# Two image layers on one core: spectral factors made on 16 partitions, squares issued at the end of a tick, buffer slots returned one tick later

## The chip, the cores and the metric

The kernel runs on one core of one Trainium2 chip. The engines of a core are PE (TensorE, matrix multiply; its weight loads are shown as PEld), DVE (VectorE), ACT (ScalarE), POOL (GpSimd) and SP (SyncE, which here only issues transfers). The metric is the device time of one execution in microseconds (us), as the median of several runs; less is better.

## The reference

The input is 8 images of 8 channels of 512 x 512, float32. Two layers follow each other, each added to its own input:

```
# layer 0
xs = group_norm(x)[:, :, ::2, ::2]
F  = rfft2(xs)                     # 8 rows (first 4, last 4) x 4 columns are kept
out2[:4 rows]  = einsum('bixy,ioxy->boxy', F[:4 rows],  w1)
out2[-4 rows:] = einsum('bixy,ioxy->boxy', F[-4 rows:], w2)
x = x + real(out2 . E1(X) . E2(T)) / 256**2    # E: complex exponentials

# layer 1, on v = group_norm(x)
grid = v
repeat 15 times:
    mapped = 3.9 * grid * (1 - grid)
    grid = 0.85 * (0.7 * mapped + 0.3 * conv3x3(mapped, K)) + 0.15 * v
cml = clip(grid, 0.0001, 0.9999)
nca = sigmoid(conv1x1(relu(conv3x3(v, Wp)), Wu))           # 128 hidden channels
g   = sigmoid(conv1x1(relu(conv3x3([v, cml, nca], Wg1)), Wg2))
x = x + g * cml + (1 - g) * nca
```

## The kernel before, in words

Everything is unrolled, and each engine keeps the order in which the source issues its instructions (`keep_order`). Time is cut into ticks: `work` (L889) issues one tick, 75 of them for each image, after a prologue that makes layer 0 of image 0. A tick holds work of several images at once: the 15 coupled steps and the hidden layer (`nca`) of image b, the gates of image b-1, and layer 0 (`layer0`, the spectral part) of image b+1. The last image has no successor, and after it only hidden rounds and gates are left.

**The steps.** A `Half` is four of the eight channels of an image. The 512 rows are covered by 19 overlapping slabs of 32 rows; five sets (k = 0 to 4) of four slabs each make a half. A tick does two (set, step) pairs, numbered n within the half: pair n is set n % 5 at step n // 5 + 1. The 75 pairs of the first half are followed directly by those of the second, and those by the next image's. `convolve` (L528) does a set's 3 x 3 convolution on PE: 48 matrix multiplies, 96 in the trace, in 3.3 us, so two sets are 192 instructions (L533). `settle` (L582) reads the result with DVE (L588), adds the drive term and squares on ACT (L594), in two pieces of two banks. The four pairs of PSUM banks turn between the two sets, the hidden rounds, and the others.

**What a half needs at its start.** Each set has two arrays of drive values, dE and dO (1 MB each, four transfers each, L491), and a state m. `fetch` (L506) issues the loads, from 11 pairs ahead of the half's start on, in the order k, then dE before dO, for as long as there are loads left and a slot is free. `square` (L510) makes the first m of a set from dE: POOL writes two border columns (L512), ACT squares 2048 columns (L513, 1.99 us). For set k it is issued in the tick that holds pair k - 2. `prepare` and `drive` (L526, POOL) scale dO and dE.

**Slots.** dE, dO and m share 15 slots of a pool, handed out first in, first out (`Slots`, L138). A drive is given back by `settle` at steps 14 and 15. At step 15 `leave` (L565) clips m on DVE (L568) and puts `store` off to the end of the tick (`later(1, ...)`, run by `tick`, L171): four transfers of the finished rows to `cml` (L574), after which the slot of m is given back at once. Who takes such a slot next, a load on SP or a memset on POOL, waits for the stores to land.

**The order within a tick** (L889 to L912): `prepare` of the halves; the two sets' `convolve` and `settle`; the gates' `finish`; `transfers`, which issues the loads of gates (`feed`), of x for layer 0, and of the halves (`fetch`); one or two hidden rounds (L633 on PE, ACT L639 and DVE L641, each on half of the result); then `squares`; then one slot of "others" (a gate's convolution L703 or a piece of layer 0), the hidden layer's point convolution every second round (L652; its result is copied to y by ACT, L659, or added by DVE, L661, and finished by ACT's sigmoid, L665), another slot of "others" (a gate's second convolution L720 or a piece of layer 0); then `tick`, which issues what was put off.

**The spectral part.** `layer0` is a generator of pieces. It projects the subsampled image with matrix multiplies on a table of cosines and sines (L336, `dft_y`, with the image as weights), normalises the sums (L350, L353), projects again (L361) to 8 partitions (one for each wave number along one axis), and mixes the channels on DVE with the weights `wmix` (`total`, L369; results `re` and `im`). The way back multiplies with e1, whose partitions 0 to 7 hold the cosines and 8 to 15 the sines. Its factors `om` therefore have 16 partitions. DVE writes the first 8 (L387, L388) and a small tile `of_sin` (L389, L390), which a transfer of 2 KB carries to partitions 8 to 15 (L391, on SP's queue). `over_rows` (L398) multiplies om by e1; ACT copies the result to ty (L402); `synthesis` (L430, L433) ends the way back. All SP transfers are issued in the order of the source; an issue that must wait holds up those behind it.

Of the kernel before, what the change touches and what calls it, by code (L numbers as in the profile page):

```python
# [35 lines left out]
F32 = mybir.dt.float32  # L36
AF = mybir.ActivationFunctionType
ALU = mybir.AluOpType
# [3 lines left out]
P = 128  # L42
C = 8
# [42 lines left out]
def shape_constants():  # L86

    ky = np.array([0, 1, 2, 3, -4, -3, -2, -1])
    kx = np.arange(4)
    c = {}  # L90
    p, j = np.arange(P)[:, None, None], np.arange(2)[None, :, None]
    a = 2 * np.pi * ((ky * (2 * p + j)) % NS) / NS
    c["dft_y"] = np.concatenate([np.cos(a), -np.sin(a)], axis=2)
    a = 2 * np.pi * ((kx * (P * j + p)) % NS) / NS
    re = np.concatenate([np.cos(a), -np.sin(a)], axis=2)
    im = np.concatenate([np.sin(a), np.cos(a)], axis=2)
    c["dft_x"] = np.stack([re, im], axis=2)
    waves = np.zeros((8, 4))
    waves[:, 0] = ky / NS
    waves[:, 1] = np.concatenate([kx, -kx]) / NS  # L100
    waves[:4, 2] = 0.25
    c["waves"] = waves
    i, o = np.arange(P)[:, None] % SLAB, np.arange(SLAB)[None, :]
    c["shift"] = np.stack([i - o == d - 1 for d in range(3)], axis=1)
    p = np.arange(P)
    c["ends"] = np.stack([p % SLAB == 0, p % SLAB == SLAB - 1, p == 0, p == P - 1], axis=1)
    c["group_of"] = (np.arange(P)[:, None] % C) // 2 == np.arange(G)[None, :]
    return {k: np.ascontiguousarray(v, dtype=np.float32) for k, v in c.items()}
# [18 lines left out]
def conv_layers(ctx: ExitStack, tc: tile.TileContext, a, out):  # L127
# [50 lines left out]
    def load(name, shape):  # L178
        t = cp.tile(shape, F32, name=name)
        nc.scalar.dma_start(out=t, in_=a[name])  # L180
        return t
# [7 lines left out]
    xs_first = [load_x(sets, 0, c) for c in range(C)]  # L189


    dft_y = load("dft_y", [P, 2, 16])
    dft_x = load("dft_x", [P, 2, 2, 8])
    waves = load("waves", [8, 4])
    group_of = load("group_of", [P, G])
    ends = load("ends", [P, 4])
    w_p = load("w_p", [P, 3, 2, HID])
# [18 lines left out]

    e1 = cp.tile([16, N], F32, name="e1")
    e2 = cp.tile([P, N], F32, name="e2")
    om = cp.tile([16, C, 32], F32, name="om")
    nc.gpsimd.memset(om, 0.0)  # L220
    grid = {}
    for name in "XT":
# [3 lines left out]
    def sines():  # L226
        u, k, t = (sets.take([8, N], name) for name in ("u", "k", "sines"))
        rd = sm.tile([8, 1], F32, name="rd")
        for to, name, col, shift in (
            (e1[:8], "X", 0, 0.25), (t, "X", 0, 0.0), (e2[:8], "T", 1, waves[:, 2:3])  # L230
        ):
            xr = grid[name]
            nc.vector.tensor_tensor(rd, xr[:, 2:3], xr[:, 0:1], ALU.subtract)
            nc.vector.reciprocal(rd, rd)
            nc.vector.tensor_tensor(rd, rd, waves[:, col : col + 1], ALU.mult)
            nc.vector.tensor_scalar(u, xr, rd, shift, ALU.mult, ALU.add)
            nc.vector.tensor_scalar(k, u, MAGIC, None, ALU.add)
            nc.vector.tensor_scalar(k, k, MAGIC, None, ALU.subtract)
            nc.vector.tensor_tensor(u, u, k, ALU.subtract)
            nc.scalar.activation(to, u, AF.Sin, scale=6.283185)  # L240
        nc.scalar.dma_start(out=e1[8:], in_=t)
        for j in range(1, 4):
            nc.scalar.dma_start(out=e2[32 * j : 32 * j + 8], in_=e2[:8])
        for tile_ in (u, k, t, *grid.values()):
            sets.drop(tile_)
# [72 lines left out]
    def layer0(e, bank):  # L318


        def one():
            return bank[-1][:, 0]

        st = sm.tile([P, C, 4, 6], F32, name="st")
        mys = sm.tile([P, C, 2, 16], F32, name="mys")


        for c in range(C):
            yield c
            xt = e.x[c]  # L330
            for j in range(4):
                nc.vector.bn_stats(st[:, c, j], xt[:, j])
            my = one()[:, :32].rearrange("p (h k) -> p h k", h=2)
            for h in range(2):
                for j in range(2):
                    nc.tensor.matmul(  # L336
                        my[:, h], xt[:, 2 * j, h * NS : (h + 1) * NS : 2], dft_y[:, j],
                        start=(j == 0), stop=(j == 1),
                    )
            nc.scalar.copy(mys[:, c], my)  # L340
            e.done_with(c)
# [6 lines left out]
        for g in range(G):  # L348
            at = mys[:, 2 * g : 2 * g + 2]
            nc.vector.tensor_scalar(  # L350
                at[:, :, :, 0], at[:, :, :, 0], lift[:, g : g + 1], None, ALU.subtract
            )
            nc.vector.tensor_scalar(at, at, rstd[:, g : g + 1], None, ALU.mult)  # L353
        wmix, ts = row([8, 2, C, C, 4], "wmix"), row([8, 2, C, C, 4], "ts")
        nc.sync.dma_start(out=wmix, in_=a["wmix"])
        yield LATER
        mx = one()[:, : C * 8].rearrange("p (c k) -> p c k", k=8)
        for c in range(C):
            for h in range(2):
                for q in range(2):  # L360
                    nc.tensor.matmul(  # L361
                        mx[:8, c], mys[:, c, h, q * 8 : (q + 1) * 8], dft_x[:, h, q],
                        start=(h + q == 0), stop=(h + q == 2),
                    )
        f = sm.tile([8, C, 2, 4], F32, name="f")
        nc.vector.tensor_copy(f, mx[:8].rearrange("p c (q k) -> p c q k", q=2))


        def total(q0, v0, q1, v1, op, name):  # L369
            for i, (q, v) in enumerate(((q0, v0), (q1, v1))):  # L370
                nc.vector.tensor_tensor(
                    ts[:, i], f[:, :, q].unsqueeze(2).to_broadcast([8, C, C, 4]), wmix[:, v],
                    ALU.mult,
                )
            nc.vector.tensor_tensor(ts[:, 0], ts[:, 0], ts[:, 1], op)
            t = sm.tile([8, C, 4], F32, name=name)
            nc.vector.tensor_reduce(t, ts[:, 0].rearrange("k i o m -> k o m i"), AX.X, ALU.add)
            return t

# [2 lines left out]
        yield LATER  # L382
        im = total(0, 1, 1, 0, ALU.add, "im")

        of_sin = sm.tile([8, C, 8], F32, name="of_sin")
        s = 1.0 / (NS * NS)
        nc.vector.tensor_scalar(om[:8, :, 0:4], re, s, None, ALU.mult)  # L387
        nc.vector.tensor_scalar(om[:8, :, 4:8], im, s, None, ALU.mult)  # L388
        nc.vector.tensor_scalar(of_sin[:, :, 0:4], im, -s, None, ALU.mult)  # L389
        nc.vector.tensor_scalar(of_sin[:, :, 4:8], re, s, None, ALU.mult)  # L390
        nc.sync.dma_start(out=om[8:, :, :8], in_=of_sin)  # L391
        yield LATER


        def over_rows(c):
            ps = one()
            for at in range(0, P, 32):
                nc.tensor.matmul(  # L398
                    ps[at : at + 32], om[:, c], e1, start=True, stop=True, tile_position=(0, at)
                )  # L400
            ty = row([P, P, 4], "ty")
            nc.scalar.copy(ty.rearrange("k p j -> k (p j)"), ps)  # L402
            return ty
# [68 lines left out]
    class Half:  # L472
# [31 lines left out]
                    self.square(k)  # L504

        def fetch(self, n):  # L506
            while n >= -11 and self.loads and (self.loads[0][2] or sets.free):
                self.load(nc.sync)

        def square(self, k):  # L510
            m = self.m[k] = sets.take([P, 4, NP], "m")
# [53 lines left out]
    def leave(m, k, half):  # L565

        g = m[:, :, 1 : N + 1]
        nc.vector.tensor_scalar(g, g, 0.0001, 1.0 - 0.0001, ALU.max, ALU.min)  # L568

        def store():  # L570
            for h in range(4):
                s = 4 * k + h
                lo, hi = SHARES[s]
                nc.sync.dma_start(  # L574
                    out=half.cml[1 + STARTS[s] + lo : 1 + STARTS[s] + hi, half.c0 : half.c0 + 4],
                    in_=g[32 * h + lo : 32 * h + hi],
                )
            sets.drop(m)

        later(1, store)  # L580

# [307 lines left out]
    def work(sets, rounds, e, after, transfers, squares=lambda: None):  # L889

        settled = iter(())
        for (half, step, k), ps in zip(sets, (pairs[:2], pairs[2:])):
            convolve(half.m[k], half.c0, step - 1, ps)
            next(settled, None)
            settled = settle(half, step, k, ps)
            next(settled)
            others.finish()
        others.finish()
        transfers()
        for ps in (pairs[:2], pairs[2:])[:rounds]:  # L900
            e.hidden.round(ps, after, settled)
        next(settled, None)
        squares()

        a, b, c, d = (pairs[i] for i in ((0, 1, 3, 2), (2, 0, 3, 2))[rounds == 1])

        point = rounds and e.hidden.n % 2 == 0
        others.first([a, b if point else c])
        if point:
            e.hidden.point(c[:, 0])  # L910
        others.second([d if point else c])
        tick()  # L912

    elements = [e]
    for n in range(-FIRST_ROUNDS, 0, 2):
# [99 lines left out]
```

## Time and profile before

| | |
|---|---|
| median of 3 runs | 9992.99 us (9989.27 to 10003.49) |
| the profiled execution | 9988.58 us; its span, first to last instruction, 9986.8 us |
| granted TensorE clock, mean | 0.983 of full |
| HBM | 992.27 MB read, 268.78 MB written, 126 GB/s over the span |

In the rows of the profile, a group is given as line, engine, operation, tiles written and read, shape and count; then busy us, mean ns of one; then the engine's idle time just before, and what ended most of it. In the views of waits each row has the us in total, the times, and the longest. In the timeline each row has start and length in us, engine, line, operation, count, and in brackets the idle time before it and what ended it. "issue" there means that the engine waited for nothing that the profile shows. PE's matrix multiplies overlap each other and their ends are modelled.

### The profile page before, as it was taken

Reading aid. Unit: us, or ns where it says so; the run is one execution under the profiler, and the core shown is the slowest. Engines: PE = TensorE matmul, PEld = TensorE weight load, DVE = VectorE, ACT = ScalarE, POOL = GpSimd, SP = SyncE. Lnnn points to the kernel's source line nnn. Section 1 sums busy time; section 2 is a strip of 40 time slices with the busy share of each in tenths; the row PEclk is TensorE's granted clock in tenths of the full one; section 3 lists DMA queues with packets and bytes.
Section 4 is the critical chain, followed back from the end, with each engine's and each line's share of the span. In section 5 each row is a group of like instructions: output and inputs, shape, how many; then the busy total and the mean of one; then the engine's idle time right before and its main releaser. Section 6 shows DMA issues by size and latency. Waiting matters only on the chain. (4 is left out here: it accounts for less than half of the span.)

```text
span 9986.8 us, 353049 instructions
## 1 busy us (share of the span) xinstructions
PE 9359.6 (94%) x160496; PEld 4296.7 (43%) x160496; DVE 5869.1 (59%) x6067; ACT 4297.8 (43%) x4445; POOL 1755.5 (18%) x1406
## 2 busy tenths in 40 slices
PE   6999999899998999989999899999999899998999
PEld 2444444443444444444444444444434444444433
DVE  5665555665566655666556655566555565555555
ACT  2444444444444434444344443444434354344422
POOL 2010111103121031101312013120121202211212
PEclk9999999999999999999999999999999999999999
DMA  4241355447544565445665356552566526753688
GB/s 147 88 120 34 82 140 134 134 127 168 139 128 136 126 163 137 133 124 135 159 144 141 112 141 162 141 158 94 143 160 145 155 91 144 168 129 94 150 199 200
DMA packets 625562, 1353.48 MB, mean 136 GB/s; under 512 B 73066, under 2 KB 73194, under 8 KB 594050
## 3 DMA queue, kind: packets, MB, share of 16 engines
q1 hardware_dynamic: 621728, 1329.77, 52.0%
q8 instruction: 1261, 20.66, 0.9%
q14 instruction: 235, 1.93, 0.1%
q10 hardware_dynamic: 2338, 1.13, 0.0%
HBM read 992.27 MB, written 268.78 MB: 126 GB/s over the span
## 5 line engine op out<-in xcount | busy, mean ns | idle before, releaser
L533 PE MATMUL pair<-m,band 32*32 32x512 f32 x115200 | 4096.7, 605 | 200.2 <-issue 96.0
L594 ACT ACTIVATE m<-m 128x1024 f32<-128x1024 f32 x2240 | 2363.7, 1055 | 2795.7 <-DVE m L588 2674.2
L533 PEld LDWEIGHTS pair<-m,band 32*32 32x32 f32 x115200 | 2262.4, 103 | 1941.3 <-issue 970.0
L633 PE MATMUL pair<-cols,w_p 32*128 32x511 f32 (+1 forms) x24576 | 2866.2, 603 | 41.4 <-DMA cols<-xn 14.2
L588 DVE SCALAR_TENSOR_TENSOR m<-pair,dO 128x1024 f32<-128x1024 f32 x1280 | 1507.2, 1219 | 1478.0 <-PE pair L533 1294.2
L633 PEld LDWEIGHTS pair<-cols,w_p 32*128 32x128 f32 x24576 | 1270.8, 186 | 1651.0 <-issue 1123.3
L588 DVE SCALAR_TENSOR_TENSOR m<-pair,dE 128x1024 f32<-128x1024 f32 x1120 | 1319.1, 1219 | 1068.6 <-PE pair L533 878.3
L641 DVE TENSOR_SCALAR h<-pair,b_p 128x1024 f32<-128x1024 f32 x1024 | 1312.9, 1283 | 810.8 <-PE pair L633 803.3
L639 ACT ACTIVATE h<-pair,b_p 128x1024 f32<-128x1024 f32 x1024 | 1140.3, 1114 | 1043.4 <-PE pair L633 1043.0
L652 PE MATMUL pair<-h,w_u 128*32 128x512 f32 x8192 | 996.5, 598 | 136.4 <-DVE h L641 123.5
L726 POOL TENSOR_TENSOR mix<-mix 96x512 f32<-96x512 f32 x344 | 437.4, 1271 | 3757.9 <-ACT mix L724 3551.2
L703 PE MATMUL pair<-gin,w_g 128*32 128x511 f32 (+1 forms) x8256 | 964.1, 600 | 33.3 <-DMA gin<-nca 17.0
L708 POOL TENSOR_TENSOR mix<-mix 96x512 f32<-96x512 f32 x344 | 443.4, 1289 | 2050.6 <-DMA mix<-nca 1340.1
L598 POOL TENSOR_SCALAR dO<-dO 128x2048 f32<-128x2048 f32 x80 | 431.9, 5410 | 1225.6 <-DVE m L588 1225.5
L652 PEld LDWEIGHTS pair<-h,w_u 128*32 128x32 f32 x8192 | 249.4, 110 | 757.1 <-issue 384.0
L703 PEld LDWEIGHTS pair<-gin,w_g 128*32 128x32 f32 x8256 | 235.3, 110 | 711.2 <-issue 472.2
L665 ACT ACTIVATE y<-y,b_u 128x512 f32<-128x512 f32 x256 | 184.7, 721 | 808.0 <-DVE y L661 807.8
L731 DVE SCALAR_TENSOR_TENSOR mix<-mix,back 96x512 f32<-96x512 f32 x344 | 335.7, 976 | 148.5 <-POOL mix L726 148.5
L659 ACT COPY y<-pair 128x512 f32<-128x512 f32 x256 | 149.7, 585 | 605.1 <-PE pair L652 482.8
L713 DVE TENSOR_SCALAR mix<-pair,b_g 128x512 f32<-128x512 f32 x344 | 258.0, 750 | 251.6 <-PE pair L703 251.4
L720 PE MATMUL pair<-mix,w_g 128*32 128x512 f32 x2064 | 356.8, 593 | 9.6 <-DVE mix L713 7.8
L526 POOL TENSOR_SCALAR dO<-dO,base 128x512 f32<-128x512 f32 x320 | 237.0, 756 | 453.8 <-DMA dO<-xn 323.0
(86 smaller groups left out, 2643.8 us busy)
## 6 DMA issues: line engine op xcount, KB each, us to landing
gin<-xn SPq DMA_DIRECT2D x344, 384.0 KB
cols<-xn SPq DMA_DIRECT2D x256, 512.0 KB
x<-in_x SPq DMA_DIRECT2D x120, 1024.0 KB
gin<-cml SPq DMA_DIRECT2D x344, 320.0 KB
gin<-nca SPq DMA_DIRECT2D x344, 320.0 KB
dE<-xn SPq DMA_DIRECT2D x320, 256.0 KB
dO<-xn SPq DMA_DIRECT2D x320, 256.0 KB
mix<-xn SPq DMA_DIRECT2D x344, 192.0 KB
```

The source lines that it names most:

```text
L533: nc.tensor.matmul(ps[h // 2][32 * t : 32 * t + 32, h % 2], band[at, c0 + (t if step % 2 else h), dx], m[at, t, dx : dx + N], start=(n == ...
L588: nc.vector.scalar_tensor_tensor(u[:, at], ps[q], FLOOR, d[:, at], ALU.max, ALU.add)
L594: nc.scalar.square(u[:, at], u[:, at])
L598: nc.gpsimd.tensor_scalar(d, d, 0.5, None, ALU.add)
L633: nc.tensor.matmul(ps[g // 2][:, g % 2, lo:hi], w_p[p, dx, i % 2], self.cols[p, i // 2, at : at + hi - lo], start=(n == 0), stop=(n == 2), ...
L639: nc.scalar.activation(h[:, :2], ps[0], AF.Relu, bias=b_p)
L641: nc.vector.tensor_scalar(h[:, 2:], ps[1], b_p, 0.0, ALU.add, ALU.max)
L652: nc.tensor.matmul(ps[32 * g : 32 * g + 32], w_u[:, r % 4], h[:, g], start=(r == self.hs[0][0]), stop=(r == self.hs[-1][0]), tile_position ...
L703: nc.tensor.matmul(ps[32 * j : 32 * j + 32, lo:hi], gband[:, dx], gin[:, j, at : at + hi - lo], start=(n == 0), stop=(n == 2), tile_positi ...
L708: nc.gpsimd.tensor_tensor(d, d, ng, ALU.subtract)
L720: nc.tensor.matmul(ps[at], gpoint[:, at], mix[:, 3], start=True, stop=True, tile_position=(0, 32 * j),)
L726: nc.gpsimd.tensor_tensor(d, d, mix[: GR * C, 2], ALU.mult)
```

## The change

Four things are changed.

1. The cosine and sine columns of `dft_y` stand twice, so both projections give their results on 16 partitions, the second 8 a copy of the first. `wmix` comes twice as well. `om` is then written whole by DVE, in four operations with per-partition scale factors (two more columns in `waves`) that are zero on one half of the partitions; the tile `of_sin` and its transfer are gone. `om` holds 8 columns for each channel in place of 32, and the matrix multiply reads 32 columns from there on, of which the first 8 are used.
2. The slot of a stored m is given back one tick after its stores are issued.
3. `squares` is called after `tick` in place of after the hidden rounds.
4. `fetch` issues at most 8 loads for each half and tick.

```diff
-    c["dft_y"] = np.concatenate([np.cos(a), -np.sin(a)], axis=2)
+    c["dft_y"] = np.concatenate([np.cos(a), np.cos(a), -np.sin(a), -np.sin(a)], axis=2)
...
-    waves = np.zeros((8, 4))
-    waves[:, 0] = ky / NS
-    waves[:, 1] = np.concatenate([kx, -kx]) / NS
+    waves = np.zeros((16, 5))
+    waves[:8, 0] = ky / NS
+    waves[:8, 1] = np.concatenate([kx, -kx]) / NS
     waves[:4, 2] = 0.25
+    waves[:8, 3] = 1.0 / (NS * NS)
+    waves[8:, 4] = -1.0 / (NS * NS)
...
-    om = cp.tile([16, C, 32], F32, name="om")
+    om = cp.tile([16, C + 3, 8], F32, name="om")
...
-        mys = sm.tile([P, C, 2, 16], F32, name="mys")
+        mys = sm.tile([P, C, 2, 32], F32, name="mys")
...
-            my = one()[:, :32].rearrange("p (h k) -> p h k", h=2)
+            my = one()[:, :64].rearrange("p (h k) -> p h k", h=2)
...
-                at[:, :, :, 0], at[:, :, :, 0], lift[:, g : g + 1], None, ALU.subtract
+                at[:, :, :, 0:9:8], at[:, :, :, 0:9:8], lift[:, g : g + 1], None, ALU.subtract
...
-        wmix, ts = row([8, 2, C, C, 4], "wmix"), row([8, 2, C, C, 4], "ts")
+        wmix, ts = row([16, 2, C, C, 4], "wmix"), row([16, 2, C, C, 4], "ts")
...
-                        mx[:8, c], mys[:, c, h, q * 8 : (q + 1) * 8], dft_x[:, h, q],
+                        mx[:16, c], mys[:, c, h, q * 16 : (q + 1) * 16], dft_x[:, h, q],
...
-        of_sin = sm.tile([8, C, 8], F32, name="of_sin")
-        s = 1.0 / (NS * NS)
-        nc.vector.tensor_scalar(om[:8, :, 0:4], re, s, None, ALU.mult)
-        nc.vector.tensor_scalar(om[:8, :, 4:8], im, s, None, ALU.mult)
-        nc.vector.tensor_scalar(of_sin[:, :, 0:4], im, -s, None, ALU.mult)
-        nc.vector.tensor_scalar(of_sin[:, :, 4:8], re, s, None, ALU.mult)
-        nc.sync.dma_start(out=om[8:, :, :8], in_=of_sin)
+        on_cos, on_sin = waves[:, 3:4], waves[:, 4:5]
+        back = sm.tile([16, C, 4], F32, name="back_re")
+        nc.vector.tensor_scalar(back, re, on_sin, -1.0, ALU.mult, ALU.mult)
+        nc.vector.tensor_scalar(re, re, on_cos, None, ALU.mult)
+        nc.vector.scalar_tensor_tensor(om[:, :C, 0:4], im, on_sin, re, ALU.mult, ALU.add)
+        nc.vector.scalar_tensor_tensor(om[:, :C, 4:8], im, on_cos, back, ALU.mult, ALU.add)
...
-                    ps[at : at + 32], om[:, c], e1, start=True, stop=True, tile_position=(0, at)
+                    ps[at : at + 32], om[:, c : c + 4].rearrange("p c k -> p (c k)"), e1, start=True, stop=True, tile_position=(0, at)
...
         def fetch(self, n):
-            while n >= -11 and self.loads and (self.loads[0][2] or sets.free):
-                self.load(nc.sync)
+            for _ in range(8):
+                if n >= -11 and self.loads and (self.loads[0][2] or sets.free):
+                    self.load(nc.sync)
...
-            sets.drop(m)
+            later(1, lambda: sets.drop(m))
...
         next(settled, None)
-        squares()
...
         others.second([d if point else c])
         tick()
+        squares()
...
-        "wmix": w12.transpose(2, 4, 0, 1, 3),
+        "wmix": np.tile(w12.transpose(2, 4, 0, 1, 3), (2, 1, 1, 1, 1)),
```

More of the change, by code (lines that the diff above doesn't have):

```diff
@@ L189, in conv_layers @@
     xs_first = [load_x(sets, 0, c) for c in range(C)]
-    dft_y = load("dft_y", [P, 2, 16])
+    dft_y = load("dft_y", [P, 2, 32])
     dft_x = load("dft_x", [P, 2, 2, 8])
-    waves = load("waves", [8, 4])
+    waves = load("waves", [16, 5])
     group_of = load("group_of", [P, G])
@@ L229, in sines @@
         for to, name, col, shift in (
-            (e1[:8], "X", 0, 0.25), (t, "X", 0, 0.0), (e2[:8], "T", 1, waves[:, 2:3])
+            (e1[:8], "X", 0, 0.25), (t, "X", 0, 0.0), (e2[:8], "T", 1, waves[:8, 2:3])
         ):
@@ L234, in sines @@
             nc.vector.reciprocal(rd, rd)
-            nc.vector.tensor_tensor(rd, rd, waves[:, col : col + 1], ALU.mult)
+            nc.vector.tensor_tensor(rd, rd, waves[:8, col : col + 1], ALU.mult)
             nc.vector.tensor_scalar(u, xr, rd, shift, ALU.mult, ALU.add)
@@ L361, in layer0 @@
                     nc.tensor.matmul(
-                        mx[:8, c], mys[:, c, h, q * 8 : (q + 1) * 8], dft_x[:, h, q],
+                        mx[:16, c], mys[:, c, h, q * 16 : (q + 1) * 16], dft_x[:, h, q],
                         start=(h + q == 0), stop=(h + q == 2),
                     )
-        f = sm.tile([8, C, 2, 4], F32, name="f")
-        nc.vector.tensor_copy(f, mx[:8].rearrange("p c (q k) -> p c q k", q=2))
+        f = sm.tile([16, C, 2, 4], F32, name="f")
+        nc.vector.tensor_copy(f, mx[:16].rearrange("p c (q k) -> p c q k", q=2))
         def total(q0, v0, q1, v1, op, name):
@@ L371, in total @@
                 nc.vector.tensor_tensor(
-                    ts[:, i], f[:, :, q].unsqueeze(2).to_broadcast([8, C, C, 4]), wmix[:, v],
+                    ts[:, i], f[:, :, q].unsqueeze(2).to_broadcast([16, C, C, 4]), wmix[:, v],
                     ALU.mult,
@@ L375, in total @@
             nc.vector.tensor_tensor(ts[:, 0], ts[:, 0], ts[:, 1], op)
-            t = sm.tile([8, C, 4], F32, name=name)
+            t = sm.tile([16, C, 4], F32, name=name)
             nc.vector.tensor_reduce(t, ts[:, 0].rearrange("k i o m -> k o m i"), AX.X, ALU.add)
```

## The prediction

> **What bounds the kernel now.** I read the busy totals first, then the waits of PE, then two stretches of the timeline. The totals name the engine:
>
> ```profile
> span 9986.8 us, 353049 instructions
> PE 9359.6 (94%) x160496; PEld 4296.7 (43%) x160496; DVE 5869.1 (59%) x6067; ACT 4297.8 (43%) x4445; POOL 1755.5 (18%) x1406
> L533 PE MATMUL pair<-m,band 32*32 32x512 f32 x115200 | 4096.7, 605 | 200.2 <-issue 96.0
> ```
>
> PE is idle for 627 us (9986.8 - 9359.6). The change takes no work from PE, so only these 627 us, and the clock that PE is granted, can give or take time. The waits of PE, longest in total first, say who owns them:
>
> ```profile
> PE pair L652 <- DVE h L641: 123.5, 140, 1.6
> PE pair L398 <- DMA om<-of_sin: 117.1, 8, 24.4
> PE pair L533 <- issue: 96.0, 58, 5.2
> PE pair L533 <- ACT m L513: 64.8, 20, 10.6
> ```
>
> The columns are us in total, times, longest. The first row is not touched. The second (the om transfer) and the fourth (the squares) are what the change is about. The third is idle time with no wait. The timeline around one om transfer:
>
> ```profile
> 1839.42 1.92 PE L652 MATMUL pair<-h,w_u 128*32 128x512 f32 x16 [1.53 <-DVE h L641]
> 1841.21 0.59 DVE L390 TENSOR_SCALAR of_sin<-re 8x32 f32<-8x32 f32 x1
> 1850.89 0.77 SPq L391 DMA_DIRECT2D om<-of_sin  x1
> 1856.48 1.20 PE L398 MATMUL pair<-e,om 16*32 16x512 f32 x4 [15.13 <-DMA om<-of_sin]
> 1857.49 8.20 PE L533 MATMUL pair<-m,band 32*32 32x512 f32 x183
> ```
>
> The factors were ready at 1841.80. Their transfer was issued 9.1 us later, behind loads in SP's queue, and landed 5.5 us after that. PE stood for all of it. The convolutions that follow took 8.20 us; the same 192 instructions take 6.58 elsewhere. Now the squares at a half's start:
>
> ```profile
> 1249.44 3.88 ACT L513 ACTIVATE m<-dE,mhalf 128x2048 f32<-128x2048 f32 x2
> 1249.92 1.93 PE L652 MATMUL pair<-h,w_u 128*32 128x512 f32 x16 [1.52 <-DVE h L641]
> 1251.77 6.58 PE L533 MATMUL pair<-m,band 32*32 32x512 f32 x192
> 1251.90 0.69 DVE L661 TENSOR_TENSOR y<-y,pair 128x512 f32<-128x512 f32 x1 [2.13 <-PE pair L652]
> 1253.22 0.71 ACT L665 ACTIVATE y<-y,b_u 128x512 f32<-128x512 f32 x1
> 1263.12 3.88 ACT L513 ACTIVATE m<-dE,mhalf 128x2048 f32<-128x2048 f32 x2
> 1265.16 8.18 PE L533 MATMUL pair<-m,band 32*32 32x512 f32 x192 [4.03 <-ACT m L513]
> ```
>
> At 1249 the squares run beside L652's matmuls and PE goes on at once. At 1263 they come last in the tick and PE stands 4.03 us, and again the convolutions after it are slow (8.18). So a square that comes late is paid in full, and with interest.
>
> [...]all eight idle stretches of 4.0 us at L533 are followed by 3.4 to 6.8 us at half clock.[...]PE stops inside a convolution at 3618.6 for 5.25 us, and a 16 KB instruction packet runs from 3620.8 to 3622.4.
>
> **The change, part by part.** Each sum is made in the profiled execution (span 9986.8, execution 9988.6; the median of the runs, 9993.0, is 4.4 above it). Aligning the two orders of instructions, PE's and POOL's are unchanged, DVE has four operations for four, ACT's squares move, and SP loses eight transfers and has loads moved.
>
> *The om transfer goes.* Idle before L398 outside the prologue: 15.1, 24.3, 18.8, 17.6, 15.1, 16.3 and 3.0, together 110. DVE now writes om itself, on 16 partitions with the same row length, so at about the same time as the last of the four old operations (1841.8, when PE was free at 1841.3): 0.6 stays at each of 7 places. Gain 106. The half clock behind the six long stretches goes too: the windows show 0.91 over 18 us, then 0.86, 0.88, 0.89, 0.88 and 0.90 over 19 each, some 2.1 us each: 13. In the prologue the transfer costs 2 (issued 62.0, L398 at 64.2).
>
> *The squares move behind the tick's other work.* ACT's order gives five cases:
> - First half, k = 0 and 1, all 8 images: now behind the sigmoid L665, which waits for L661, which waits for the end of L652. From the rows above: 1252.58 + 0.06 + 0.71 + 1.99 = 1255.3 for the first square, where PE began at 1251.77. +3.5, 8 times: 28.
> - First half, k = 4, behind the copy of y (L659, 0.58), 7 places: PE would go on at 1281.2 in place of 1280.16. +1.1: 8.
> - Second half, k = 1 and 2, behind the copy of ty (L402) and the sigmoid, 6 images: L661 ends 1875.79, so the square ends 1878.5; PE went on at 1876.51. With what PE had done before, +2.1, and +3.0 in image 0: 16.
> - Second half, k = 3 and 4, behind the copy of y, 7 places: 1891.8 + 0.58 + 1.99 = 1894.4 for 1891.69. +2.7: 19.
> - Second half, k = 0, is first used by the second set of the next tick, one convolution of 3.3 us later: hidden, with 0.7 to spare; beyond that it costs us for us. k = 2 and 3 of the first half have nothing behind them and do not move.
>
> Sum 71, all on PE. Behind each late square PE's whole queue waits, so nothing takes it up.
>
> *The half clock that these draw.* Stretches of 3.5 to 3.9 (cases one and three, 15 places): after 4.0 us the convolutions took 8.0 to 9.3 for 6.58, so 1.9 each, 28. Stretches of 2.6 to 2.8 (14 places): about six in ten such stretches of this trace drew one, so 1.1 each, 16. Together 44; bounds 20 and 73.
>
> *Slots and loads.* At the second half's start four sets were loaded in one tick, two of them into slots whose stores SP had only just issued; now two, and two a tick later, into slots stored a tick earlier. At the first half three become two, and the cap of 8 moves the last dO one tick further: SP issues it behind y's store and ahead of the renewals, and POOL's L526 waits for it with drives and the memset of k = 4 queued behind. I see some 6 us of slack there and cost it nothing; if it lands later, PE loses that excess, at up to 8 places. In the last image the memset L512 waited for stores until 9071.29 and PE stood 10.57; now one slot comes from a dO freed by DVE, so PE stands about 3.5[...], and less half clock follows: gain 8 (3 to 10). In the prologue y's next copy waited 8.67 us for y's store, behind 24 loads; the store now passes 8 of them: PE's 3.4 idle at 175.3 and part of a half clock, gain 7 (0 to 10). Smaller bursts elsewhere: 2 (0 to 8).
>
> *Instruction fetch.* The bytes stay, so the 107 us of busy DMA in which PE stood at L398 are now worked through. In the six stretches PE lost 25 us in about 220 us of full DMA outside those waits, 0.115 a us: 12, and 7 of half clock. Together 19 (5 to 35).
>
> *Wider operands.* L336 streams 32 columns for 16, 512 times. L652's 598 ns for 512 columns gives 19 ns: at most 10 us, least 0, since its weight load (212 ns) already runs beside it. I take 3. DVE's and ACT's widening (L353, L340) is under 0.1 us an instruction beside PE work.
>
> **Sum.** Gains 106 + 13 + 2 + 8 + 7 + 2 = 138. Costs 71 + 44 + 19 + 3 = 137. Net -1 on 9988.6, so 9988 in this execution's terms and 9992 in the median's. A measurement of this kernel tells about 0.2% (20 us) from no change.
>
> **Rivals.**
> - *Faster.* [...]fetch keeps up because fewer loads stand in the queue. Half clock 20 (not 44), fetch 5: costs 99 against 138, -39: 9954. For it: stretches of 2.2 and 2.6 at 1828 and 5498 drew no half clock. Against: those of 3.4 and more in the steady part all did.
> - *Slower, by the half clock alone.* Five of the eight 4.0 us stretches drew 6.8 us of half speed, not 3.4. If all 29 new places cost 2.5, that is 73: +28: 10021. Above 2.2 a place it passes 20 us. For it: the first case is preceded by another 1.5 us idle before L652[...].
> - *The change doesn't do what it says.* The 15 us at L398 hid the DMA backlog, and without them PE meets a load or store that is late (the memset of k = 2, the last dO): the om gain of 119 is replaced by a new wait. +118: 10110. Against it: the last of the loads moved are needed 6 us or more after I expect them to land.
>
> **How the numbers follow.** The balance as summed (within 20 us): 0.40. Faster: 0.25. Slower by the clock: 0.28; by a new DMA wait, whole or in part: 0.07. The likeliest case's own range is 9972 to 10012. From the other two it reaches to 9950 and 10040, which leaves about 2 in 10 outside. So faster 0.25, same 0.40, slower 0.35.
>
> **What would show it.** Right: no wait of L398 for a transfer, and waits of L533 for ACT m L513 grown from 65 to about 130 us; convolutions of over 8 us behind most of them; L533's "issue" idle up by some 12. Wrong: if the waits on L513 stay near 65 the kernel is clearly faster; if waits of POOL's L512 or L526 for transfers stand before late squares, the backlog decides.

## The result, and the profile after

The changed kernel takes 9962.79 us (median of 6 runs, 9953.04 to 9967.33) where the kernel before took 9991.13 beside it: ratio 0.9967, 95% interval 0.9957 to 0.9977, so 23 to 43 us less. The forecast was 9992, no change. The result lies inside the forecast's outer range (9950 to 10040), but below the range of its main case (9972 to 10012), and nearer to its "faster" rival (9954). In the profiled executions the span went from 9986.8 to 9954.7, 32.1 us less. The page of the changed kernel (its lines of code stand three to five further down than before: L533 is now L537, L513 is L517, L398 is L401):

```profile
span 9954.7 us, 353098 instructions
PE 9377.2 (94%) x160496; PEld 4306.9 (43%) x160496; DVE 5869.8 (59%) x6067; ACT 4303.2 (43%) x4445; POOL 1763.8 (18%) x1406
L537 PE MATMUL pair<-m,band 32*32 32x512 f32 x115200 | 4120.7, 609 | 269.8 <-ACT m L517 135.4
```

PE is busy 17.6 us longer for the same 160496 multiplies, most of it because it ran more of them at half clock (23 us more, which costs 12); it is idle 50 us less. (The mean granted clock rose from 0.983 to 0.987 all the same, since it counts idle time too, and before, the clock stood at half for 84 us of the om waits, while PE did nothing.) The waits of PE (us in total, times, longest):

```profile
PE pair L537 <- ACT m L517: 135.4, 41, 5.5
...
PE pair L537 <- issue: 100.3, 61, 4.8
...
PE pair L637 <- issue: 13.7, 9, 2.7
```

The 117 us for om's transfer are gone. The squares' wait has doubled, from 64.8 to 135.4 us (forecast: about 130). Two places of the timeline, the late square of a first half and the former om wait:

```profile
1254.48 0.69 DVE L665 TENSOR_TENSOR y<-y,pair 128x512 f32<-128x512 f32 x1 [2.13 <-PE pair L656]
1255.20 0.72 ACT L669 ACTIVATE y<-y,b_u 128x512 f32<-128x512 f32 x1 [3.39 <-DVE y L665]
1255.83 3.88 ACT L517 ACTIVATE m<-dE,mhalf 128x2048 f32<-128x2048 f32 x2
1257.87 6.65 PE L537 MATMUL pair<-m,band 32*32 32x512 f32 x150 [3.45 <-ACT m L517]
...
1853.25 0.23 DVE L393 SCALAR_TENSOR_TENSOR om<-im,waves,back_re 16x32 f32<-16x32 f32 x1
1853.54 0.63 PE L401 MATMUL pair<-e,om 16*32 16x512 f32 x4 [0.57 <-DVE om L393]
```

ACT had nothing to do for 3.39 us ahead of the sigmoid, in which the square could have run; it stood behind it. PE pays 3.45 (forecast 3.5). At om, 0.57 is left of 15.1 (forecast 0.6).

The table sorts PE's idle time by what ended it, for the kernels that the next section needs. "Idle" is time in which PE runs neither a multiply nor a weight load. "Idle, all" and "half speed" are of the whole span, the three rows between them of the time after the first 210 us. "No wait" is idle in front of the convolutions, the hidden rounds and other multiplies that the profile calls issue; the om wait, which it also books there in part, stands by itself. "Half speed" is the time in which PE worked at a granted clock of half. It is priced here at half of itself, an estimate from the trace of the changed kernel: two sets' 192 convolution instructions, run without a pause, took 8.15 us with 3.3 to 3.5 us at half clock (median of 18 places) and 6.58 without any (478 places), so 1.57 more for about 3.4. All are summed from the traces.

| us | before | changed | om_alone | squares_alone | cap_alone | om_and_cap | best_cap_early |
|---|---|---|---|---|---|---|---|
| span | 9986.8 | 9954.7 | 9899.4 | 10086.3 | 9889.4 | 9861.4 | 9847.0 |
| idle, all | 618.2 | 568.7 | 537.2 | 691.6 | 526.6 | 511.6 | 493.9 |
| at over_rows, for om | 110.2 | 4.9 | 14.7 | 105.1 | 46.6 | 14.7 | 14.7 |
| convolutions, for a square | 60.9 | 127.8 | 64.5 | 139.2 | 50.6 | 52.7 | 9.8 |
| no wait | 125.1 | 134.9 | 151.4 | 134.3 | 122.0 | 144.2 | 162.2 |
| half speed | 223.3 | 246.6 | 209.6 | 297.4 | 203.0 | 178.1 | 170.5 |

### The profile page after: what moved, and what is told of

Its sections match the earlier page's. It is cut to its first block, busy times and chain, and to the rows that moved or that the text cites. A ratio compares the mean times of both kernels' runs of the same rounds, so it can differ in the third digit from the quotient of the medians.

```text
span 9954.7 us, 353098 instructions
## 1 busy us (share of the span) xinstructions
PE 9377.2 (94%) x160496; PEld 4306.9 (43%) x160496; DVE 5869.8 (59%) x6067; ACT 4303.2 (43%) x4445; POOL 1763.8 (18%) x1406
## 3 DMA queue, kind: packets, MB, share of 16 engines
q8 instruction: 1261, 20.66, 0.9%
## 5 line engine op out<-in xcount | busy, mean ns | idle before, releaser
L537 PE MATMUL pair<-m,band 32*32 32x512 f32 x115200 | 4120.7, 609 | 269.8 <-ACT m L517 135.4
L537 PEld LDWEIGHTS pair<-m,band 32*32 32x32 f32 x115200 | 2270.4, 104 | 2026.3 <-issue 1002.7
L656 PE MATMUL pair<-h,w_u 128*32 128x512 f32 x8192 | 992.8, 596 | 135.4 <-DVE h L645 119.6
```

The source lines that it names most:

```text
L537: nc.tensor.matmul(ps[h // 2][32 * t : 32 * t + 32, h % 2], band[at, c0 + (t if step % 2 else h), dx], m[at, t, dx : dx + N], start=(n == ...
L656: nc.tensor.matmul(ps[32 * g : 32 * g + 32], w_u[:, r % 4], h[:, g], start=(r == self.hs[0][0]), stop=(r == self.hs[-1][0]), tile_position ...
```

## The experiments

The change has four parts: om without a transfer, squares at the tick's end, the late return of stored slots, and the cap of 8 loads. Late return with the squares in the middle was not tried: by the author's count the pool of 15 slots runs out there; om_and_hold below comes nearest to it. Differences below are (ratio - 1) times 9990, against the kernel before on the same chip. Where two runs come from different chips, their differences are compared and not their medians.

| run | om | late squares | late return | cap | median us | ratio (95%) | difference |
|---|---|---|---|---|---|---|---|
| changed | x | x | x | x | 9963 | 0.9967 (0.9957-0.9977) | -33 |
| om_alone | x | | | | 9909 | 0.9918 (0.9905-0.9932) | -82 |
| squares_alone | | x | | | 10083 | 1.0088 (1.0074-1.0101) | +88 |
| cap_alone | | | | x | 9890 | 0.9895 (0.9881-0.9909) | -105 |
| om_and_squares | x | x | | | 9958 | 0.9964 (0.9952-0.9976) | -36 |
| no_cap | x | x | x | | 9967 | 0.9975 (0.9966-0.9983) | -25 |
| cap_without_late_return | x | x | | x | 9936 | 0.9950 (0.9937-0.9963) | -50 |
| om_and_cap | x | | | x | 9865 | 0.9871 (0.9858-0.9884) | -129 |

**om_alone.** The changed kernel with these three edits undone:

```diff
-            for _ in range(8):
-                if n >= -11 and self.loads and (self.loads[0][2] or sets.free):
-                    self.load(nc.sync)
+            while n >= -11 and self.loads and (self.loads[0][2] or sets.free):
+                self.load(nc.sync)
...
-            later(1, lambda: sets.drop(m))
+            sets.drop(m)
...
         next(settled, None)
+        squares()
...
         tick()
-        squares()
```

> The kernel before with only the first part of the change: om made by DVE on 16 lines, no transfer; squares, slots and loads as before. Theory T (the sum: the om wait 106 and its half clock 13 come back in full, the prologue 2, instruction fetch takes at most 19 back): 100 to 121 us faster than before, so 9870 to 9891. Rival R1 (the 15 us waits at over_rows also let the backlog of transfers drain, and in the change the late squares took over that service): without the late squares the loads and instruction fetches stop PE elsewhere, and no more than 60 us come: 9931 or more, with new transfer waits or issue idle above 130 us in the trace. Rival R2 (the change's 28 us came from the slots and loads, and om and squares cancel): om gives 119 less 0 to 10 here too, so it is told apart from T by the other three runs.

Measured: 82 us less (68 to 95), between the two theories. Waits of PE:

```profile
PE pair L536 <- issue: 119.4, 58, 5.2
PE pair L536 <- ACT m L516: 69.7, 21, 12.5
...
PE pair L401 <- DVE om L393: 20.0, 8, 5.3
```

Of the om wait's 105 us that went in the changed kernel, 96 go here, and 26 come back as idle without a wait (125.1 to 151.4). This is instruction fetch: of the 45 such stretches of over 1.5 us in this trace (after the first 250 us), 43 have a 16 KB packet of the instruction queue under way, and PE goes on 1.44 us after its end (median; 42 of the 43 within 1.26 to 1.63). That a packet is under way could be chance in about half of the cases (an estimate: this trace has 1261 such packets of 1.17 us, one in 7.85 us, and a stretch lasts 2.8 us); the fixed delay could not. In 38 of the 45 the DMA engines are more than 0.9 busy from 5 us before the stretch to its end; of windows of 8 us taken at random only about one in six is so full. So R1's mechanism, transfers that stop PE elsewhere, is there, at about half of the size that R1 gave it.

The third row is a surprise. At six places PE now waits 2.2 us for om, in the changed kernel 0.6. In the timeline:

```profile
1829.59 2.21 POOL L529 TENSOR_SCALAR dE<-dE,base_e 128x512 f32<-128x512 f32 x2 [2.28 <-ACT m L516]
...
1829.70 0.61 DVE L391 TENSOR_SCALAR re<-re,waves 16x32 f32<-16x32 f32 x1
...
1830.34 1.49 DVE L392 SCALAR_TENSOR_TENSOR om<-im,waves,re 16x32 f32<-16x32 f32 x1
1831.76 0.23 DVE L393 SCALAR_TENSOR_TENSOR om<-im,waves,back_re 16x32 f32<-16x32 f32 x1
1832.05 0.63 PE L401 MATMUL pair<-e,om 16*32 16x512 f32 x4 [2.20 <-DVE om L393]
```

L392 takes 1.49 us at all six and ends with POOL's drive; in the changed kernel, with a late square and so a late drive, it takes 0.24 at all six. So L392 takes 1.25 us more with the drive beside it; at the place shown both end at 1831.8. In what way the one holds up the other is not shown.

**squares_alone.** The kernel before with only the call moved behind `tick()`.

> The kernel before with only the squares moved behind the tick's other work; the om transfer stays, slots and loads as before. Theory T: 71 us of new idle and 33 to 44 us of half clock, in all 100 to 115 us slower: 10091 to 10106, waits of the convolutions for the squares near 135 us. Rival R3 (the places draw little half clock when nothing else is changed, or the squares' delay partly falls into the om waits that are still there): 70 to 80 us slower, 10061 to 10071.

Measured: 88 us more (74 to 101), between T and R3. The waits of PE:

```profile
PE pair L533 <- ACT m L513: 146.8, 41, 12.3
...
PE pair L398 <- DMA om<-of_sin: 112.1, 8, 22.4
PE pair L533 <- issue: 100.6, 57, 3.9
```

The squares' own idle is T's (60.9 to 139.2 in the table, +78), and the om wait stays; half speed rises by 74, which costs 37. The profiled execution is the longest of four, so its 99.5 us of span is above the median's difference.

**om_and_squares, no_cap and cap_without_late_return.** The changed kernel without the two slot edits, without the cap alone, and without the late return alone (edits as in the diff above).

> The changed kernel with the two slot edits undone (a stored set's slot is given back at once, loads not capped). Theory T: the slot edits together are worth 17 us (last image 8, prologue 7, smaller 2), so this runs 10 to 20 us longer than the changed kernel (9963): 9973 to 9983, with the 10.6 us wait of the last image and the 3.4 us wait for y's copy in the prologue back. Rival R2 (the slots and loads brought the 28 us or more): 9990 or more. Rival R4 (the slot edits do nothing): 9958 to 9968.

> The changed kernel without the cap of 8 loads a tick; the slot of a stored set still comes back a tick later. Theory T: the cap binds in the prologue and for one dO of each first half only; the prologue's 3.4 us of idle and part of a half clock come back, so 0 to 10 us longer than the changed kernel: 9963 to 9973. Rival R5 (the cap spreads the loads and so is what kept the instruction fetch from growing): 10 to 25 us longer, 9973 to 9988, with issue idle at the convolutions up by 8 or more.

> The changed kernel with a stored set's slot given back at once; cap, late squares and om as changed. It completes the table: om and squares alone gave -32 us against before, with the late return -23, with both slot edits -28. Theory F2 (with late squares their pauses serve the transfers already, and neither slot edit matters): 9950 to 9970. Rival F4 (the late return costs what the cap brings, and the cap without it would bring its 43 us here too): 9915 to 9940.

Measured: -36, -25 and -50. The first is R4's: with late squares the two slot edits together bring nothing that can be told from zero, although the last image's long wait is back without them. The second is T's. The third falls in F4's range by its median, but its interval (37 to 63) meets that of the changed kernel (23 to 43). Whether the late return costs some 15 us is left open.

What stands out is that om_and_squares is -36 where the two parts alone add to +6. In the traces the second of the two parts meets less: the squares add 78 us of waiting on top of om as well (64.5 to 142.9), but PE stops 18 us less for fetch (151.4 to 132.9), 10 less for om, and not at all for ty (6.1 before). These 34 us explain the missing 42 only in part: the profiled execution of om_and_squares is its longest, 21 us above the median, and its time at half speed rises by 103 us over om_alone's, where squares_alone added 74.

**om_and_cap and om_and_hold.** om without a transfer and squares in the middle, once with the cap and once with another brake: in om_and_hold a load may not take a slot that was stored in the last tick, a square may.

```diff
 class Slots:
+        self.fresh = 0          # stored in the last tick; store() adds 1, a tick later takes it back
...
-            while n >= -11 and self.loads and (self.loads[0][2] or sets.free):
+            while n >= -11 and self.loads and (self.loads[0][2] or len(sets.free) > sets.fresh):
```

> om without a transfer and at most 8 loads a tick; the squares stay in the middle of the tick and a stored set's slot comes back at once. It asks why om alone lost some 30 us of its 119 to instruction fetch (idle without a cause at the convolutions 120 us for 96 before, with half clock behind it) while the changed kernel lost none. Theory F1 (the burst of 16 loads in one tick at a second half's start crowds the fetch out): with 8 and 8 the idle falls to 108 or less and the time by 12 or more against om alone (9909), to 9897 or less. Theory F2 (the pauses that the late squares make are when the fetch catches up): the idle stays at 115 or more and the time within 8 us of 9909.

> om without a transfer, squares in the middle of the tick, no cap; loads may not take a slot that was stored in the last tick, but the squares still may (the late return of slots, for loads alone). Theory F1: as with the cap, 9897 or less, idle without a cause at 108 or less; and the 12.5 us wait of the last image for a store stays, since the squares still take such slots. Theory F2: idle 115 or more, within 8 us of 9909.

Measured: the cap brings 47 us more than om alone (82 to 129), the hold 10, which is not clear of noise (ratio 0.9908, 0.9895 to 0.9921). F1's time came true for the cap, but not by F1's figure. The waits with the cap:

```profile
PE pair L537 <- issue: 110.7, 65, 4.8
PE pair L537 <- ACT m L517: 57.9, 19, 5.5
```

Issue idle falls only from 119.4 to 110.7. The other parts are 12 us of waits for squares (the last image's 12.49 becomes 3.84: its slot's store lands earlier) and 16 us of half clock. The hold takes the same 12 off the squares, though the last image's wait was expected to stay (12.49 becomes 2.94), and the stops for fetch grow by 7 (151.4 to 158.4 of idle without a wait). It still issues 12 loads in one tick at a first half's start, where the cap issues 8. That this burst is the difference is argued, not shown.

**om_late_second_half.** As om_alone, with the squares at the tick's end for the second half only.

```diff
-        squares()
+        squares(False)      # all but the second half's
...
         tick()
+        squares(True)       # the second half's
```

> om without a transfer, with the squares at the tick's end for the second half only; those of the first half in the middle, slots and loads as before. Theory F2: idle without a cause at the convolutions falls to 108 or less near the second halves' starts and takes back 10 to 20 us of the 35 us of new idle and some 17 of half clock that these squares cost: 20 to 42 us above om alone, 9929 to 9951. Theory F1: it stays near 120 and the squares are paid in full: 52 or more above, 9961 or more.

Measured: 9923 (ratio 0.9929, 0.9916 to 0.9942), 11 above om alone by the ratios and 14 by the medians, less than F2 said; F1's 9961 is out. These squares add 43 us of waiting (64.5 to 107.2) and take back 10 at om, 6 at ty and 7 at the fetch. A late square is thus paid in full where it stands, but what would have stopped PE next is then partly over.

**cap_alone.** The kernel before with only the cap.

> The kernel before with only the cap of 8 loads a tick. Theory F1 (bursts of loads crowd out the instruction fetch and hold up stores, whatever else is done): 15 to 43 us faster than before, 9948 to 9976, the 117 us at over_rows shorter too, since om's transfer stands behind fewer loads. Rival F3 (the cap pays only where om's transfer no longer interrupts the loads): within 10 us of before, 9981 to 10001.

Measured: 105 us less (91 to 119): more than F1's most, and more than the whole change. The wait for om's transfer and its place in the timeline:

```profile
PE pair L398 <- DMA om<-of_sin: 53.5, 8, 11.0
```

```profile
1825.71 2.19 SPq L491 DMA_DIRECT2D dE<-xn  x4
1827.95 6.54 SPq L491 DMA_DIRECT2D dO<-xn  x4
...
1832.62 0.16 DVE L390 TENSOR_SCALAR of_sin<-re 8x32 f32<-8x32 f32 x1
1835.30 0.77 SPq L391 DMA_DIRECT2D om<-of_sin  x1
...
1842.49 1.20 PE L398 MATMUL pair<-e,om 16*32 16x512 f32 x4 [10.97 <-DMA om<-of_sin]
```

Before, the same tick had this in SP's queue between y's store and om's transfer:

```profile
1832.09 3.00 SPq L491 DMA_DIRECT2D dE<-xn  x4
...
1835.13 5.76 SPq L491 DMA_DIRECT2D dO<-xn  x4
...
1841.48 3.94 SPq L491 DMA_DIRECT2D dE<-xn  x4
...
1846.38 3.45 SPq L491 DMA_DIRECT2D dO<-xn  x4
```

Sixteen loads stood ahead of om's 2 KB, now eight: it is issued 2.5 us after its data are ready (1832.78 to 1835.30) in place of 9.1. At the six places the delay before the issue falls from 8 to 16 us to 0 to 2.8. From the issue to PE's start it still takes 3.7 to 7.2 us (5.6 to 8.0 before), and 2.0 in image 0, where no load stands ahead (issued at 350.0). The six long waits, 15 to 24 us before, are now 4 to 11. Together 64 of the 110 us go, by an edit in one function, without touching the spectral part. To issue om's transfer ahead of the loads, or from another engine, was not tried.

**om_hold_early_square.** As om_and_hold; the first half's squares of k = 2 and 4 are issued between the settling of the tick's two sets.

```diff
+        def early(self, n):
+            for k in (2, 4):
+                if k - 2 == n and sets.free:
+                    self.square(k)
...
-            next(settled, None)
+            if settled:
+                next(settled, None)
+                early()
             settled = settle(half, step, k, ps)
```

> As om_and_hold, and of the first half's squares those of k = 2 and k = 4 are issued on ACT earlier in their tick, between the settling of the tick's first set and that of its second, ahead of the hidden rounds' copies. In om alone PE waits 4.03 us for the square of k = 2 at 8 places and 1.55 for that of k = 4 at 7. Theory E: the first shrinks to about 1.4 (then PE waits for ACT's and DVE's reading of the hidden round, which the earlier square delays by 0.6) and the second by 1.0: 21 + 7 idle, and half clock behind the first shrinks by 0 to 16: 28 to 44 us below om_and_hold. Rival (the earlier square delays the reading of the hidden round by its own 2 us, and PE waits there instead): 0 to 10 below.

Measured: 9875, 32 below om_and_hold, which is E's. The place that cost 4.03 us:

```profile
1243.74 1.99 ACT L521 ACTIVATE m<-dE,mhalf 128x2048 f32<-128x2048 f32 x1
...
1249.37 1.11 ACT L652 ACTIVATE h<-pair,b_p 128x1024 f32<-128x1024 f32 x1 [0.44 <-PE pair L646]
...
1250.63 6.69 PE L541 MATMUL pair<-m,band 32*32 32x512 f32 x192 [1.29 <-ACT h L652]
1251.33 1.99 ACT L521 ACTIVATE m<-dE,mhalf 128x2048 f32<-128x2048 f32 x1
```

The first square is done at 1245.7, before the hidden round's copy starts at 1249.4, and is not in its way; the second has until the set after. The waits for squares fall from 52.2 to 10.7.

**best_cap_early and best_plus_late_k0.** om, cap, squares in the middle and the early squares together; and the same with the second half's k = 0 square at the tick's end, so that POOL's drive leaves DVE's om operations alone.

> The candidate to beat both kernels: om without a transfer, cap of 8 loads a tick, squares in the middle of the tick, slots given back at once, and of the first half the squares of k = 2 and k = 4 earlier in their tick (as in om_hold_early_square). Theory: the cap was worth 43 us over om alone and the early squares 32 over om_and_hold; they work on different waits, so they add: 9865 - 32 = 9833 (9822 to 9845). Rival (what the early squares free is taken by the instruction fetch, whose idle rose by 13 us in om_hold_early_square): 9850 to 9865.

> As best_cap_early, with one square more moved: that of the second half's k = 0, to the tick's end as in the change. In the runs with squares in the middle PE waits 2.2 us at over_rows for DVE's om at 6 places, in those with late squares 0.5: POOL's drive of dE follows the square and runs beside DVE's four small om operations, which then take up to 1.49 us for 0.2. Theory: 10 us of idle and some 5 of half clock go, the late square leaks 4.8 as in the change: 5 to 15 us below best_cap_early. Rival (DVE's om operations are slow for another reason): 0 to 10 us above it.

Measured: 9848 (ratio 0.9857, 0.9844 to 0.9871) and 9845 (0.9856, 0.9840 to 0.9873); both beat the kernel before and the changed one.

```profile
span 9847.0 us, 353169 instructions
PE 9344.0 (95%) x160496; PEld 4287.1 (44%) x160496; DVE 5875.1 (60%) x6067; ACT 4299.2 (44%) x4445; POOL 1762.8 (18%) x1406
```

```profile
PE pair L542 <- issue: 115.6, 71, 4.2
PE pair L542 <- ACT h L648: 42.0, 39, 7.8
```

The first gains 14 us over om_and_cap by the ratios and 17 by the medians, where 32 were expected and 0 to 15 by its rival: the squares' waits fall by 43, but idle without a wait rises by 18 and the wait for the hidden round's copy from 25.7 to 42.0. The second does what it was made for (the om wait falls from 14.7 to 6.0, and L392 takes 0.24 at all six places), so it was POOL's drive beside it that made L392 slow; the 5 to 15 us expected of it are not seen: the two times cannot be told apart.

## Why the prediction was right, and where its steps were off

The forecast's sum was -1, the profiled executions differ by -32. So the change was right to be called small, because the two large terms, om and the squares, were each right to a few us and nearly cancel. But the miss of 31 us is more than the 20 that the main case allowed itself, and the "faster" rival (-39) came nearer. Step by step:

- *om.* Forecast 106 of idle and 13 of half clock; measured 105.3 (110.2 to 4.9) and 12.9 (25.7 us at half speed behind it, none now). DVE's four operations take 0.23 to 0.24 us each on 16 partitions; the old four, on 8, had means of 0.16, 0.17, 0.22 and 0.59. Right as a term of this change. As the value of the edit it is not: om_alone gained 82 and om on top of the cap 24 (105 to 129). The sum gave no hint of that, since it priced each edit in the presence of the others.
- *Squares.* Forecast 71. The late squares bring 76 us of waiting: 3.45 at eight places of the first half and at seven of the second, 2.6 at seven, and 1.0 to 1.5 more than before at seven. They take away 5 that PE had waited for ty, so 71 it is. (The table shows 67: the last image's gain of 7 is in it, and 2 fall into the first 210 us.) The cover of 0.7 us for the second half's k = 0 held at all six places: four stops of 0.5 to 1.6 us in those convolutions end 1.2 to 1.5 us after a 16 KB instruction packet and belong to the fetch.
- *Their half clock.* Forecast 44. Time at half speed behind squares rose from 51.6 to 118.3 us, which costs 33. The 15 stretches of 3.5 us cost 1.7 each and not 1.9 (1.4 at the first half's eight, 2.0 at the second half's seven), so 25 for 28. Of the 14 of 2.6 us, 8 drew a half clock, in all 12 for 16. The remaining 4 went at places that stood before as well, most of it in the last image. Two readings behind this term were a little high: of the 15 stretches of 2.4 to 3.0 us in the trace before (after the first 250 us), 7 and not six in ten are followed by half clock, and of the eight of 4.0 us, four and not five drew 6.8 us. The "faster" rival's 20 was an estimate; the 33 lie between it and the 44.
- *Instruction fetch.* This is the term that failed: forecast 12 of idle and 7 of half clock. The transfers ran full where it said so: in the trace before, the DMA share is 1.06 from 1807 to 1823, 0.99 to 1841 and 1.01 to 1857. Measured +10 of idle without a wait (125.1 to 134.9), but 17 us less at half speed behind such stretches, worth -9: together about +1 in place of +19. The mechanism is real, for om_alone shows 26 of idle. What the prediction had wrong is that nothing takes up the pauses of the late squares: with om's transfer gone, squares at the tick's end leave 18 us less of idle without a wait (om_alone to om_and_squares), those of the second half alone 7 (om_late_second_half). The "faster" rival had the small fetch term, but not its reason, fewer loads in the queue: om_and_squares has the loads uncapped and stands at 132.9 as well. These are single traces, and squares_alone shows no such fall (125.1 to 134.3), but there the om waits still made pauses of their own (105.1).
- *Slots and loads.* Forecast 17 for the last image, the prologue and smaller bursts. The last image gave 7 of idle; the prologue about 6 (1.5 of idle, 9.3 us less at half speed); the many small waits 15 in place of 2, with 4 of half clock elsewhere against it. In the changed kernel this is near by its trace, but the runs do not confirm it: with late squares, those with and without both edits cannot be told apart (-33 and -36). What the step did not see is the cap's worth in other company: 105 alone, 47 on top of om, because it was priced only at places where it binds once om's transfer is gone.
- *Wider operands.* Forecast 3; the busy time of L336 went from 77.4 to 78.5 and that of L361 from 14.3 to 14.8, so 1.6. One L340 went from 178 to 205 ns and one L353 from 257 to 289.

The measured parts make 36 of the 32 us: some 4 us of PE's longer busy time stay without an account. The miss is mostly fetch (18), half clock of the squares (11) and small waits. The "new DMA wait" rival did not happen in the changed kernel, but its mechanism is seen in om_alone: with om's wait gone and squares in the middle, a memset at 1849.6 waits for a store and PE 3.3 us behind it.

## What to carry to other kernels

Price a part of a change also alone and in pairs: two edits that remove the same wait do not add (om 82 and cap 105 made 129), and a bundle can hide that one of its parts costs more than the rest brings (with om and cap, the squares at the tick's end cost some 80 us: om_and_cap -129, cap_without_late_return -50). Before removing a small transfer on a critical chain, look at what stands ahead of it in its queue; here a limit of eight loads a tick was worth at least as much as taking the transfer away (105 and 82). Work that is ready early should stand in its in-order queue ahead of work that still waits for another engine, at the first moment when its engine is idle; here two squares issued earlier in their tick brought 32 us (om_hold_early_square).

## What the runs showed of the hardware

- Time won back on PE while the transfers ran full went in part to instruction fetch: idle without a wait rose from 125 to 151 us (om_alone) and from 144 to 162 us (best_cap_early against om_and_cap). Most instruction packets came without a long stop: om_alone fetched 1261 of 16 KB, and PE stopped for more than 1.5 us without a wait 45 times. But such a stop lasted up to 5.2 us, and PE went on about 1.4 us after the packet's end.
- Behind pauses for a square PE's clock went to half the more often, the longer they were: in the changed kernel after 8 of 14 of 2.6 us, 13 of 15 of 3.5 us and all eight of 4.0 us, for 3.4 or 6.8 us each time.
- Two small DVE operations on 16 x 32 elements, 0.24 us each by themselves (changed kernel), took about 0.6 and 1.49 beside a POOL tensor_scalar on 128 x 512, at 6 of 6 places (om_alone).
